# Small constants on another queue at the start, and the last tokens ahead of the feed-forward weights

## The chip, the cores and the metric

The kernel runs on one core of one Trainium2 chip. The metric is the device time of one launch in microseconds (us); lower is better. All tensors are float32. The core has five engines that each work through their own list of instructions in order: TensorE (PE in profiles), VectorE (DVE), ScalarE (ACT), GpSimd (POOL) and SyncE (SP), which here only issues transfers (DMAs). DMAs issued by SP and by ScalarE and by GpSimd stand in three queues; in the profile these are q1 (SP), q10 (ScalarE) and q0 (GpSimd).

## The reference

The input x has 4 sequences of 1024 tokens with 512 channels. Four blocks follow one another, each added to its input:

```python
x = x + mixer_a(layernorm(x))     # 16 heads of 64, state 64
x = x + ffn(layernorm(x))
x = x + mixer_b(layernorm(x))     # 64 heads of 16, state 128
x = x + ffn(layernorm(x))         # the same weights again
```

A mixer is a state-space layer: a projection (`in_proj_w`) gives a gate z, the channels that go through a causal convolution of four taps (weights `conv_w`, bias `conv_b`) and one dt for each head. With `A = -exp(A_log)` and `dt = softplus(dt + dt_bias)` a decaying state is carried along the sequence; `D` times the channel is added, the result is gated, normalized with the weight `norm_w`, and projected by `out_proj_w`.

The feed-forward block, cut to its core, is

```python
x_norm  = layer_norm(x, in_gamma, in_beta)
thought = x_norm[:, -1, :] @ agg_w + agg_b              # the last token of each sequence
for _ in range(4):
    t = layer_norm(thought, pn_gamma, pn_beta)
    t = gelu(t @ d1_w + d1_b)
    thought = thought + (t @ d2_w + d2_b)
broadcast = (thought @ bc_w + bc_b)[:, None, :]
gate = sigmoid(x @ gate_w + gate_b)                      # all tokens
out = layer_norm(x + gate * broadcast, out_gamma, out_beta)
```

So a chain of small products on four rows (the thought) stands beside a large product on all 4096 tokens (the gates), and the result needs both.

## The kernel before, in words

The tokens are cut into 32 items of 128 (NT). `mixer` (L188) takes them in groups of two (256 tokens), and is called twice, for a and for b; `ffn` (called 0 and 1 below) is called after each. Between them the activations go through DRAM (`xa`, `xb`).

**The mixer's start.** At L221 to L242 the weights and constants are loaded. `load_big` (L136) issues a weight in pieces, by turns on SP and on GpSimd. For w_in these are five cuts of columns: the first, third and fifth on SP, the others on GpSimd. Then SP issues the small constants one after the other: cw (convolution weights, L225), cb (their bias, L227), nw (norm weight, L229), dtb (dt bias, L231), Ab (A_log given to all partitions, L233), and Dc (D, L236 to L239), whose rows are given to the partitions with a last dimension that is strided in DRAM: 1024 pieces of four bytes, in two DMAs for mixer a and eight for b. w_out (L242, 2 MB) and the x of later groups follow on SP. VectorE then scales cw and cb (L244, L245), limits Ab (L247), ScalarE takes its exponential (L248), VectorE multiplies it (L249), and w_out is scaled with nw in eight instructions (L252).

**The order in a mixer.** The instructions of PE, DVE, ACT and POOL are laid out by hand under `tc.manual_schedule`: the norm of the first group (L373 to L413: statistics, scaling xn on ScalarE, transposes tpx on TensorE, copies into xnT on ScalarE), then `front` of the first group (products pz for the gate z and pd for dt, pc for the channels, all L324 or L480; the convolution L451 on VectorE), then chunk by chunk with the next group's front dealt out between. The transfers on SP and everything in `ffn` are put in order by the scheduler of the language, from the program's own order and its cost estimates. DMAs issued by SP and ScalarE share eight completion semaphores in turn, so that a DMA is issued only when the one eight before it in that turn has landed.

**The feed-forward part.** The order of its text is the order of its priorities. L1012 to L1029 name the loads: gw (gate weights, on GpSimd), the rows gb, agb, d2b, gam, bet, bcb (on GpSimd, helper `row`, L1002), the columns ing, inb, png, pnb, d1b (on SP, helper `col`, L1007), agg (SP), d1 in four pieces of 512 columns by turns on SP and GpSimd, and d2 in two halves (d2a on SP, d2b_w on GpSimd). After the helpers comes the chain: xl, the last token of each of the four sequences, is loaded in four DMAs (L1080 to L1082), normalized twice, transposed (tpl), scaled with ing and inb, and multiplied by agg (`split_project`, L1053, agg_ps, then the sum over the partitions sum_agg). Four thought steps follow (L1092: tpt, d1_ps, hr, tph, Gelu, d_ps, sum_d). `gate(i)` (L1129) makes the gate of one item: xn, transposes tpg, copy xnT, product g_ps (L1141), sg. ffn 0 makes all 32 gates and stores them; its last part is done in mixer b, in `last_step`. ffn 1 makes 12 gates ahead, then bc_ps (L1162), the row hb through DRAM to hbc on all partitions, and for each item the last step (L1183 to L1196), with a further gate after each.

Of the kernel before, what the change touches and what calls it, by code (L numbers as in the profile page):

```python
# [8 lines left out]
F32 = mybir.dt.float32  # L9
# [6 lines left out]
P = 128  # L16
GC = 2
GT = GC * P
D = 512
KD = D // P  # L20
E = 1024
KE = E // P
FF = 2048
KF = FF // P
# [48 lines left out]
def hybrid_kernel(  # L73
# [37 lines left out]
    nc = tc.nc  # L111
    NB, S, _ = x.shape
    NCH = S // P
# [5 lines left out]
    wts = ctx.enter_context(tc.tile_pool(name="wts", bufs=1))  # L119
# [16 lines left out]
    def load_big(tag, shape, src, name, parts):  # L136

        t = wts.tile(shape, F32, tag=tag, name=name)
        v = src.rearrange("(k p) n -> p k n", p=P)
        for i, (k0, k1, n0, n1) in enumerate(parts):  # L140
            eng = nc.sync if i % 2 == 0 else nc.gpsimd
            eng.dma_start(t[:, k0:k1, n0:n1], v[:, k0:k1, n0:n1])
        return t
# [44 lines left out]
    def mixer(m, in_w, conv_w, conv_b, dt_bias, A_log, Dv, norm_w, out_w, src, dst, first, stats, last_step=None):  # L188
        NH, HD, N = m.heads, m.head, m.state
# [18 lines left out]
        with stack:  # L208
            wk = stack.enter_context(tc.tile_pool(name=f"wk_{m.name}", bufs=1, reuse_waits="tile"))
# [5 lines left out]
            def mm(name):  # L215
# [5 lines left out]
            w_in = load_big(  # L221
                "w1", [P, KD, m.cols], in_w, f"w_in_{m.name}", [(0, KD, n0, n1) for n0, n1 in cuts]
            )
            cw = wk.tile([P, m.tiles, TAPS], F32, tag="cw", name=f"cw_{m.name}")
            nc.sync.dma_start(cw, conv_w)  # L225
            cb = wk.tile([P, m.tiles], F32, tag="cb", name=f"cb_{m.name}")
            nc.sync.dma_start(cb, conv_b)  # L227
            nw = wk.tile([P, KE], F32, tag="nw", name=f"nw_{m.name}")
            nc.sync.dma_start(nw, norm_w)  # L229
            dtb = wk.tile([P, NH], F32, tag="dtb", name=f"dtb_{m.name}")  # L230
            nc.sync.dma_start(dtb, dt_bias.partition_broadcast(P))  # L231
            Ab = wk.tile([P, NH], F32, tag="Ab", name=f"Ab_{m.name}")
            nc.sync.dma_start(Ab, A_log.partition_broadcast(P))  # L233

            Dc = wk.tile([P, KE], F32, tag="Dc", name=f"Dc_{m.name}")
            d_heads = Dv.rearrange("(e h) -> h e", h=HT)  # L236
# [709 lines left out]
            with tc.manual_schedule(  # L946
# [13 lines left out]
                for n in range(len(groups)):  # L960
                    if n + 2 < len(groups):
                        fs.append(Group(*groups[n + 2]))
                    f, ahead, behind = (fs + [None, None])[n : n + 3]
# [22 lines left out]
    def ffn(r, src, dst, stats):  # L986
# [4 lines left out]
        with stack:  # L991
            wk = stack.enter_context(tc.tile_pool(name=f"wk_f{r}", bufs=1, reuse_waits="tile"))
# [9 lines left out]
            def row(src, tag, parts=P, pool=wk):  # L1002
                t = pool.tile([parts, D], F32, tag=tag, name=f"{tag}_{r}", bufs=1)
                nc.gpsimd.dma_start(t, src.partition_broadcast(parts))
                return t

            def col(src, tag, n):  # L1007
                t = wk.tile([P, n], F32, tag=tag, name=f"{tag}_{r}")
                nc.sync.dma_start(t, src)
                return t  # L1010

            d2_rows = d2_w.rearrange("(s r) n -> s r n", s=2)  # L1012
            w_d2b = wk.tile([P, KF // 2, D], F32, tag="d2b_w", name=f"d2b_w_{r}")
            w_agg = wk.tile([P, KD, D], F32, tag="aggbc", name=f"agg_{r}")
            gw = wk.tile([P, KD, D], F32, tag="gw", name=f"gw_{r}")
            nc.gpsimd.dma_start(gw, gate_w.rearrange("(k p) n -> p k n", p=P))
            gb = row(gate_b, "gb")
            ing, inb = col(in_gamma, "ing", KD), col(in_beta, "inb", KD)
            agb, d2b = row(agg_b, "agb", NB), row(d2_b, "d2b", NB)
            png, pnb = col(pn_gamma, "png", KD), col(pn_beta, "pnb", KD)  # L1020
            d1b = col(d1_b, "d1b", KF)
            nc.sync.dma_start(w_agg, agg_w.rearrange("(k p) n -> p k n", p=P))
            w_d1 = load_big("w1", [P, KD, FF], d1_w, f"d1_{r}", [(0, KD, q * D, (q + 1) * D) for q in range(FF // D)])
            w_d2 = [load_big("w2", [P, KF // 2, D], d2_rows[0], f"d2a_{r}", [(0, KE, 0, D)])]
            nc.gpsimd.dma_start(w_d2b, d2_rows[1].rearrange("(k p) n -> p k n", p=P))
            w_d2.append(w_d2b)
# [50 lines left out]
                nc.tensor.matmul(ps[:NB], sums, rows, start=True, stop=True)  # L1077
                return ps[:NB]

            xl = wk.tile([NB, D], F32, tag="row", name=f"xl_{r}")  # L1080
            for b in range(NB):
                nc.sync.dma_start(xl[b : b + 1, :], src[b * NCH + NCH - 1][P - 1 : P, :])  # L1082
            for n, eps in enumerate((1e-5, 1e-6)):
                normalize(xl, xl, layer_stats(sm, xl, eps, "l", f"l{n}_{r}"))
            tx = tnT[:, :, :NB]
# [7 lines left out]
            for s in range(4):  # L1093
                tag = f"{r}_{s}"
# [117 lines left out]

    stats = [pp.tile([P, NT, 3], F32, tag="stats", name=f"stats_{r}") for r in range(2)]
    mixer(MIX_A, a_in_w, a_conv_w, a_conv_b, a_dt_bias, a_A_log, a_D, a_norm_w, a_out_w, streams[0], streams[1], first_x, stats[0])
    step = ffn(0, streams[1], None, stats[0])
    mixer(MIX_B, b_in_w, b_conv_w, b_conv_b, b_dt_bias, b_A_log, b_D, b_norm_w, b_out_w, streams[1], streams[2], [], stats[1], step)
    ffn(1, streams[2], streams[3], stats[1])


# [65 lines left out]
```

## Time and profile before

| What | Before |
|---|---|
| Time, median of 3 runs | 3233.39 us (3232.75 to 3239.16) |
| The profiled execution's own time | 3234.7 us |
| Its span in the profile | 3233.0 us |
| Mean granted TensorE clock | 0.965 of full speed |
| TensorE busy | 2890.7 us, 89% |
| VectorE busy | 2035.7 us, 63% |
| ScalarE busy | 1246.2 us, 39% |
| GpSimd busy | 782.5 us, 24% |
| Bytes moved by DMA | 135.97 MB, mean 42 GB/s |

In the profile the stages lie as follows: mixer a to about 1228 us, ffn 0 to about 1420, mixer b to about 2962, ffn 1 to the end. Each line of the timeline gives the start, the duration, the engine, the source line, the instruction with what it writes and reads, how many of them stand in a row, and in brackets how long the engine was idle before and what released it. A line of transfers ("SPq") times only the issue on the engine's queue, not the transfer. The table of stretches gives the busy time of each engine in each stretch, so that one sees in each stage which engine is full. TensorE's records overlap a little[...].

### The profile page before, as it was taken

The numbers are of one execution on the slowest core, as the hardware profiler recorded it, in microseconds if no ns is written. First come the engines' busy times: TensorE is split into PE (matmuls) and PEld (weight loads), VectorE is DVE, ScalarE is ACT, GpSimd is POOL, SyncE is SP. The second block draws the span as 40 slices with busy tenths as digits, with TensorE's granted clock in tenths as the row PEclk, the third lists the DMA queues.
The fourth block names the chain that finished last, engine by engine and source line by source line (L and its number), as shares of the span: only waits on it lengthen the run. The fifth ranks groups of instructions, "written<-read, shape, count | busy, mean of one in ns | idle before, by whom it ended". The sixth has DMA issues, their size and how long they took to land. (4 is left out here: it accounts for less than half of the span.)

```text
span 3233.0 us, 48622 instructions
## 1 busy us (share of the span) xinstructions
PE 2890.7 (89%) x18372; PEld 1916.6 (59%) x18372; DVE 2035.7 (63%) x4326; ACT 1246.2 (39%) x2848; POOL 782.5 (24%) x842
## 2 busy tenths in 40 slices
PE   6999999999999988988999888989888989997973
PEld 5666666666666653356666666666666666664331
DVE  4666566655556642267766687776687676674288
ACT  2333333333333323334443444344444444343242
POOL 1122121122211221022222223221222222221068
PEclk9999999999999998999999999999999999998987
DMA  3000000000000025420000000000000000023143
GB/s 110 15 16 15 16 16 16 22 16 16 15 16 22 16 67 176 168 86 12 29 19 25 19 26 24 19 22 22 19 25 22 17 25 19 22 68 125 33 147 117
DMA packets 100521, 135.97 MB, mean 42 GB/s; under 512 B 40792, under 2 KB 44376, under 8 KB 100288
## 3 DMA queue, kind: packets, MB, share of 16 engines
q1 hardware_dynamic: 86944, 100.92, 10.1%
q10 hardware_dynamic: 9216, 16.78, 1.4%
q0 software_dynamic: 4128, 15.16, 1.3%
q8 instruction: 146, 2.39, 0.3%
q14 instruction: 87, 0.71, 0.1%
HBM read 96.09 MB, written 36.72 MB: 41 GB/s over the span
## 5 line engine op out<-in xcount | busy, mean ns | idle before, releaser
L324 PE MATMUL pc_b<-xnT_b,w_in_b 128*128 128x259 f32 x1280 | 360.3, 408 | 22.2 <-DVE u_b L451 22.2
L786 DVE TENSOR_TENSOR L_b<-L_b,Gm_b 128x1024 f32<-128x1024 f32 x256 | 317.4, 1282 | 2.9 <-ACT L_b L779 2.9
L646 PE MATMUL pout_a<-w_out_a,h_a 128*128 128x512 f32 x512 | 285.6, 650 | 27.3 <-DVE u_a L451 27.3
L324 PE MATMUL pc_a<-xnT_a,w_in_a 128*128 128x259 f32 x1152 | 309.2, 393 | 0.0
L324 PE MATMUL pz_a<-xnT_a,w_in_a 128*128 128x256 f32 x1024 | 300.2, 407 | 8.9 <-ACT xnT_a L413 8.9
L324 PE MATMUL pz_b<-xnT_b,w_in_b 128*128 128x256 f32 x1024 | 292.4, 394 | 0.7 <-ACT xnT_b L413 0.7
L324 PEld LDWEIGHTS pc_b<-xnT_b,w_in_b 128*128 128x128 f32 x1280 | 230.7, 201 | 101.6 <-issue 37.3
L1141 PE MATMUL g_ps<-gw,xnT_f 128*128 128x512 f32 x512 | 253.2, 639 | 39.4 <-ACT xnT_f L1138 25.5
L779 ACT ACTIVATE L_b<-seg_b 128x512 f32<-128x512 f32 x512 | 262.7, 598 | 65.9 <-PE seg_b L772 65.1
L646 PE MATMUL pout_b<-w_out_b,h_b 128*128 128x512 f32 x512 | 278.5, 635 | 0.0
L451 DVE SCALAR_TENSOR_TENSOR u_b<-pc_b,cw_b,u_b 128x256 f32<-128x256 f32 x480 | 231.7, 483 | 70.7 <-ACT u_b L447 59.3
L802 PE MATMUL py_b<-L_b,hdt_b 128*32 128x128 f32 x4096 | 162.7, 294 | 118.0 <-DVE L_b L786 116.7
L451 DVE SCALAR_TENSOR_TENSOR u_a<-pc_a,cw_a,u_a 128x256 f32<-128x256 f32 x432 | 208.3, 482 | 53.0 <-ACT u_a L447 41.6
L324 PEld LDWEIGHTS pc_a<-xnT_a,w_in_a 128*128 128x128 f32 x1152 | 193.3, 190 | 68.5 <-issue 22.9
L802 PEld LDWEIGHTS py_b<-L_b,hdt_b 128*32 128x32 f32 x4096 | 109.5, 115 | 161.7 <-issue 81.7
L1141 PEld LDWEIGHTS g_ps<-gw,xnT_f 128*128 128x128 f32 x512 | 97.4, 201 | 169.2 <-issue 116.4
L324 PEld LDWEIGHTS pz_a<-xnT_a,w_in_a 128*128 128x128 f32 x1024 | 168.6, 193 | 47.1 <-ACT xnT_a L413 9.3
L447 ACT ACTIVATE u_a<-pc_a,cb_a,cw_a 128x256 f32<-128x256 f32 x144 | 81.3, 564 | 283.9 <-PE pc_a L324 220.3
L324 PEld LDWEIGHTS pz_b<-xnT_b,w_in_b 128*128 128x128 f32 x1024 | 166.3, 190 | 37.1 <-issue 18.2
L854 POOL TENSOR_TENSOR h_b<-h_b,z_b 128x256 f32<-128x256 f32 x128 | 90.6, 729 | 386.4 <-ACT sq_b L853 386.4
L824 DVE TENSOR_TENSOR yo_a<-po_a,ea_a 128x512 f32<-128x512 f32 x56 | 36.1, 686 | 220.4 <-PE po_a L820 220.4
L647 PEld LDWEIGHTS ssq_a<-ones,sq_a 128*128 128x128 f32 x512 | 98.4, 194 | 127.8 <-issue 115.9
(310 smaller groups left out, 5275.3 us busy)
## 6 DMA issues: line engine op xcount, KB each, us to landing
x_f<-xa SPq DMA_DIRECT2D x32, 256.0 KB
sgd<-sg SPq DMA_DIRECT2D x32, 256.0 KB
sgl<-sgd SPq DMA_DIRECT2D x32, 256.0 KB
x_b<-xa SPq DMA_DIRECT2D x32, 256.0 KB
xb<-x_b ACTq DMA_DIRECT2D x32, 256.0 KB
x_f<-xb SPq DMA_DIRECT2D x32, 256.0 KB
x_g<-xb SPq DMA_DIRECT2D x32, 256.0 KB
out<-x_g SPq DMA_DIRECT2D x32, 256.0 KB
```

The lines of the kernel that those rows point to most:

```text
L324: nc.tensor.matmul(*args, **kw)
L447: nc.scalar.activation(u, ps[:, 0:GT], AF.Identity, bias=cb[:, j : j + 1], scale=cw[:, j, 0:1])
L451: nc.vector.scalar_tensor_tensor(u, ps[:, k : k + GT], cw[:, j, k : k + 1], u, ALU.mult, ALU.add)
L646: nc.tensor.matmul(pout, f.hs[e // 2][:, e % 2, cols], w_out[:, e, :], **on)
L647: nc.tensor.matmul(ssq[:, 0:1], sqs[e // 4][:, e % 4, :], ones[:, 0:1], **on)
L779: nc.scalar.activation(L[:, r], sg[r0 + r], AF.Exp)
L786: nc.vector.tensor_mul(Lr, Lr, Gm.unsqueeze(1).to_broadcast([P, 2 * HB, P]))
L802: nc.tensor.matmul(py[cg * CT : (cg + 1) * CT, e % 4, :], hdt[:, h // HC, u : u + HC, :], Ls[half][:, r, hq, :], start=not started[cg], st ...
L824: nc.vector.tensor_mul(heads_of(tmp), heads_of(po), over_head(el[:, half * HALF : (half + 1) * HALF], P, HALF))
L854: nc.gpsimd.tensor_mul(yh, yh, zs[half * 2 + r][:, :, cols])
L1141: nc.tensor.matmul(ps, xnT[:, k, :], gw[:, k, :], start=(k == 0), stop=(k == KD - 1))
```

## The change

In the mixer, Ab, cw, cb and dtb are issued first of the constants and in this order; for mixer a (`first`) they are issued by ScalarE, for mixer b by SP. nw, Dc and w_out stay where they were on SP. In `ffn`, d1 is loaded in two halves, both on SP, and named first; then gw, then the four xl loads (before, at the head of the chain), agg, and the rows and columns; d2 and the rest follow as before.

```diff
+            q = nc.scalar if first else nc.sync
+            Ab = wk.tile([P, NH], F32, tag="Ab", name=f"Ab_{m.name}")
+            q.dma_start(Ab, A_log.partition_broadcast(P))
             cw = wk.tile([P, m.tiles, TAPS], F32, tag="cw", name=f"cw_{m.name}")
-            nc.sync.dma_start(cw, conv_w)
+            q.dma_start(cw, conv_w)
             cb = wk.tile([P, m.tiles], F32, tag="cb", name=f"cb_{m.name}")
-            nc.sync.dma_start(cb, conv_b)
+            q.dma_start(cb, conv_b)
+            dtb = wk.tile([P, NH], F32, tag="dtb", name=f"dtb_{m.name}")
+            q.dma_start(dtb, dt_bias.partition_broadcast(P))
             nw = wk.tile([P, KE], F32, tag="nw", name=f"nw_{m.name}")
             nc.sync.dma_start(nw, norm_w)
-            dtb = wk.tile([P, NH], F32, tag="dtb", name=f"dtb_{m.name}")
-            nc.sync.dma_start(dtb, dt_bias.partition_broadcast(P))
-            Ab = wk.tile([P, NH], F32, tag="Ab", name=f"Ab_{m.name}")
-            nc.sync.dma_start(Ab, A_log.partition_broadcast(P))
...
+            v_d1 = d1_w.rearrange("(k p) n -> p k n", p=P)
+            w_d1 = wts.tile([P, KD, FF], F32, tag="w1", name=f"d1_{r}")
+            for n0 in range(0, FF, FF // 2):
+                nc.sync.dma_start(w_d1[:, :, n0 : n0 + FF // 2], v_d1[:, :, n0 : n0 + FF // 2])
+            gw = wk.tile([P, KD, D], F32, tag="gw", name=f"gw_{r}")
+            nc.gpsimd.dma_start(gw, gate_w.rearrange("(k p) n -> p k n", p=P))
+            xl = wk.tile([NB, D], F32, tag="row", name=f"xl_{r}")
+            for b in range(NB):
+                nc.sync.dma_start(xl[b : b + 1, :], src[b * NCH + NCH - 1][P - 1 : P, :])
+            w_agg = wk.tile([P, KD, D], F32, tag="aggbc", name=f"agg_{r}")
+            nc.sync.dma_start(w_agg, agg_w.rearrange("(k p) n -> p k n", p=P))
+            gb = row(gate_b, "gb")
+            agb, d2b = row(agg_b, "agb", NB), row(d2_b, "d2b", NB)
+            ing, inb = col(in_gamma, "ing", KD), col(in_beta, "inb", KD)
+            png, pnb = col(pn_gamma, "png", KD), col(pn_beta, "pnb", KD)
+            d1b = col(d1_b, "d1b", KF)
             d2_rows = d2_w.rearrange("(s r) n -> s r n", s=2)
             w_d2b = wk.tile([P, KF // 2, D], F32, tag="d2b_w", name=f"d2b_w_{r}")
-            w_agg = wk.tile([P, KD, D], F32, tag="aggbc", name=f"agg_{r}")
-            gw = wk.tile([P, KD, D], F32, tag="gw", name=f"gw_{r}")
-            nc.gpsimd.dma_start(gw, gate_w.rearrange("(k p) n -> p k n", p=P))
-            gb = row(gate_b, "gb")
-            ing, inb = col(in_gamma, "ing", KD), col(in_beta, "inb", KD)
-            agb, d2b = row(agg_b, "agb", NB), row(d2_b, "d2b", NB)
-            png, pnb = col(pn_gamma, "png", KD), col(pn_beta, "pnb", KD)
-            d1b = col(d1_b, "d1b", KF)
-            nc.sync.dma_start(w_agg, agg_w.rearrange("(k p) n -> p k n", p=P))
-            w_d1 = load_big("w1", [P, KD, FF], d1_w, f"d1_{r}", [(0, KD, q * D, (q + 1) * D) for q in range(FF // D)])
...
-            xl = wk.tile([NB, D], F32, tag="row", name=f"xl_{r}")
-            for b in range(NB):
-                nc.sync.dma_start(xl[b : b + 1, :], src[b * NCH + NCH - 1][P - 1 : P, :])
```

In the order that the scheduler lays out, SP issues at the start of mixer a x, the three w_in cuts, nw, Dc twice, w_out and then the next x; ScalarE issues Ab, cw, cb and dtb before its table load and takes the exponential of Ab before xn. In mixer b, ScalarE's exponential of Ab comes between the two copies into xnT, where it came after both. In both feed-forward parts SP still issues d1 at the end of the mixer, and then d2a, the four xl, agg, ing, inb, png, pnb, d1b, where it was d2a, the five columns, agg, xl. gw keeps its place on GpSimd.

## The prediction

> **What bounds the kernel now.** I read the table of stretches first, because the change touches only the start of the kernel and the ends of its mixers. Its columns are the stretch, then busy microseconds (count) of TensorE, its weight loads, VectorE, ScalarE and GpSimd, the granted clock, the DMA share and GB/s.
>
> ```profile
> 0.00:20.00 20.00, 1.97 (x8) 1.57 (x8) 5.97 (x38) 3.39 (x4) 5.25 (x15) 1.00 0.82 279
> 20.00:40.00 20.00, 19.17 (x73) 16.57 (x74) 5.93 (x17) 2.43 (x6) 0.00 (x0) 1.00 0.43 159
> 40.00:60.00 20.00, 12.38 (x60) 9.86 (x58) 17.76 (x54) 9.29 (x20) 1.40 (x4) 0.96 0.00 0
> 60.00:80.00 20.00, 20.00 (x103) 15.19 (x102) 7.10 (x17) 7.91 (x21) 1.90 (x1) 0.87 0.04 8
> 1340.00:1360.00 20.00, 20.00 (x59) 8.99 (x58) 3.46 (x5) 7.37 (x13) 0.00 (x0) 1.00 0.77 281
> 1420.00:1440.00 20.00, 18.53 (x95) 16.07 (x96) 18.41 (x58) 9.89 (x17) 2.76 (x2) 1.00 0.09 19
> 3020.00:3040.00 20.00, 19.66 (x121) 6.77 (x124) 5.64 (x15) 4.53 (x8) 0.54 (x1) 1.00 0.05 14
> 3200.00:3220.00 20.00, 0.00 (x0) 0.00 (x0) 17.95 (x30) 3.88 (x5) 17.10 (x15) 0.50 0.40 132
> ```
>
> TensorE sets the pace of both mixers and of the first feed-forward part. Exceptions: before 20 us nearly nothing runs; from 38 to 60 us VectorE does; at 1420 to 1480 VectorE does; and after 3080, when the thought chain is done, VectorE and GpSimd do. Next, the timeline of the start (start, duration, engine, line, work, idle before and what released it):
>
> ```profile
> 8.89 0.22 DVE L394 SCALAR_TENSOR_TENSOR mv_a<-mv_a 128x1 f32<-128x1 f32 x2
> 19.18 0.18 DVE L244 TENSOR_SCALAR cw_a<-cw_a 128x36 f32<-128x36 f32 x1 [10.07 <-DMA cw_a<-in_L_attn_a_conv_w]
> ...
> 35.26 3.26 DVE L252 TENSOR_SCALAR w_out_a<-w_out_a,nw_a 128x512 f32<-128x512 f32 x8 [2.89 <-DMA w_out_a<-in_L_attn_a_out_proj_w]
> 38.44 2.94 DVE L451 SCALAR_TENSOR_TENSOR u_a<-pc_a,cw_a,u_a 128x256 f32<-128x256 f32 x6
> ```
> ```profile
> 11.10 0.59 ACT L413 COPY xnT_a<-tpx_a 128x512 f32<-128x512 f32 x1 [0.50 <-PE tpx_a L411]
> 20.09 0.21 ACT L248 ACTIVATE Ab_a<-Ab_a 128x16 f32<-128x16 f32 x1 [8.40 <-DVE Ab_a L247]
> ```
> ```profile
> 7.90 4.05 SPq L233 DMA_DIRECT2D Ab_a<-in_L_attn_a_A_log x1
> 11.99 3.66 SPq L238 DMA_DIRECT2D Dc_a<-in_L_attn_a_D x2
> 19.00 0.39 SPq L142 DMA_DIRECT2D w_out_a<-in_L_attn_a_out_proj_w x1
> ```
>
> Two waits stand in a row. The small constants land only at 19 us, behind w_in; ScalarE's exponential of Ab stands between its two copies into xnT, so TensorE's first pz starts at 20.83. Then w_out lands at 35.26, and its eight scalings stand before the first convolution on VectorE, which therefore starts at 38.44 and is what the stretch to 60 us runs on.
>
> **Startup.** Ab, cw, cb and dtb move to ScalarE's queue ahead of its table load; nothing is added or removed. VectorE's order becomes Ab, statistics of x, cw, aggregate, cb, ..., so its set-up stands behind cb. SP issued three such loads in 0.45 to 1.10 us each and x_first took 2.9 us from issue (0.81) to use (3.72), so with w_in running beside it I put cb at 5 to 7 us. From 4.66 to 9.11 VectorE has 4.45 us of set-up plus 0.2 for Ab: L394 ends at 9.7 to 11.7. From there to both copies done takes 3.6 us (9.1 to about 12.5 without the exponential): TensorE starts at 13.3 to 15.3, 5.5 to 7.5 earlier.
>
> Here the Trainium skill is weighed ("DMA: Bandwidth & Descriptors"). "Rules for kernel authors" speaks against the change: loads spread over SP, ACT and GpSimd gain no bandwidth, only issue time. Then the constants would land as w_in drains, at 17.5, TensorE would start no earlier than before (17.5 + 4.65 + 3.6 = 25.7), and z would be ready at 37.2, hardly ahead of 38.44: gain about 1 us at most. "Queues, rings and completion order" says that each engine takes its rings in turn. The row decides for the latter, since GpSimd's and SP's queues did share from 8 to 12 us:
>
> ```profile
> q0 software_dynamic: 261, 1.02, 66.2%
> q1 hardware_dynamic: 266, 0.54, 36.7%
> ```
>
> But the first convolution still needs w_out, which stays on SP behind w_in and Dc. SP's issues freeze when all the loads in flight have not landed (a load waits for the eighth before it, and Ab's took 4.05 us to get in); w_out was issued only at 19.00, because the load eight before it was w_in's last. Now that place is cb's, so w_out goes out at about 7 us, and Dc at 6 to 7 instead of 12. Dc is 1024 pieces of four bytes. The same page's rule that a strided last dimension becomes one descriptor per element agrees, and would only name a cost; its size is in the trace, as packets in 19 to 22 us (first) and in 1428 to 1430 us, where Dc of mixer b has the queue to itself:
>
> ```profile
> DMA packets 283, 0.00 MB, mean 0 GB/s; under 512 B 283, under 2 KB 283, under 8 KB 283
> ...
> DMA packets 238, 0.00 MB, mean 0 GB/s; under 512 B 238, under 2 KB 238, under 8 KB 238
> ```
>
> That is 94 to 119 per us, 8.6 to 10.9 us for 1024. Yet in 17 to 18 us 946 small packets passed in one us, when w_in had just drained. So the slow part is making the pieces, not moving them, and it ran on behind w_in from 12 us. Started at 6.5 it ends at 15 to 17.5, about when w_in drains; w_out's 2 MB follow in 5.3 us (at the 390 GB/s of 8 to 12 us), plus some 2 us to land: 24 to 27, I take 26. If instead the pieces are only worked off once w_in is gone, w_out lands at about 34. I take 26 for the burst at 17 us; both ends stay in the range. First convolution: the later of w_out + 3.2 (35.26 to 38.44) = 29.2 and z done (TensorE's start + 10.85 + 0.7 = 24.9 to 26.9). So 29.2 against 38.44: **-9** (ends -11 and -1). It is kept to the end: VectorE is busy 17.8 of 20 us after its first convolution and in the same order, and TensorE saturates after that. The next x loads land behind w_out at about 28 and are first used 6 us after the first convolution (44.38 before), so they hide; third w_in waits for Ab's landing, hidden too since its columns are needed 15 us after TensorE's start.
>
> **First feed-forward part.** Both halves of d1 now go on SP (before, half on GpSimd at 0.8 us of issue each, with nothing behind them that waited). The sums' round trips through DRAM are all issued before d1, so nothing urgent is behind it. xl goes straight after d2a, then agg, then the five small constants; the last xl waits for the last store of the mixer (issued 1229.79), so agg is issued near 1232 as before. inb now waits for d2a's landing (about 1241) and is used at about 1256. The thought chain starts some 4 us earlier, but TensorE is busy 20 of 20 us up to 1380 with the same products: **0** (-1 to +1.5).
>
> **Start of mixer b.** Ab first on SP; ScalarE now does copy, table load (1.28), exponential, copy, so pz starts near 1424.3 instead of 1422.8. VectorE, with 18.4 of 20 busy, hides 1.5 us and saves waits of 0.91 and 0.33: **-0.3** (-0.9 to +1.5 if that cover is gone).
>
> **Second feed-forward part.** TensorE, one bc product, and the tail:
>
> ```profile
> 2975.42 16.27 PE L1141 MATMUL g_ps<-gw,xnT_f 128*128 128x512 f32 x32 [5.50 <-DMA gw<-in_L_ffn_gate_w]
> 2992.80 0.41 PE L1051 MATMUL tpl<-ident,xl 4*128 4x4 f32 x4 [1.12 <-DVE xl L184]
> ...
> 3071.13 3.60 PE L1162 MATMUL bc_ps<-bc,thT 128*4 128x512 f32 x8
> ```
>
> gw's load stays where it was. xl was issued at 2976.46, after d2a had landed; now at about 2964, so its norm runs before the gates' products finish and tpl comes near 2989. The same products then stand between the steps as before. Waits of TensorE for the chain go: 1.12 (tpl), 1.70, 0.28 and 0.34 (at later steps), 0.68 (3070.07), and one gate product of 0.95 moves behind bc: 5.1 at most, of which I count those that my step by step sum kept: bc ends at 3070.8 instead of 3074.7, **-3.9** (-1 to -4; the tail's different interleaving of gates and items adds -2 to +6 at its ends). The tail is bound by VectorE and GpSimd and starts when hbc lands, so it moves along.
>
> **Sum.** -9 + 0 - 0.3 - 3.9 = -13.2 from the profiled execution's 3234.7 us gives 3221.5. The median of the runs, 3233.39, is 1.3 lower: **3220.2**. The measurement can tell 0.2%, 6.5 us.
>
> **Rivals.** (1) w_out takes the place of the constants: it lands at 34, the startup gives 1 and the sum is -5.2: 3228. For it: Dc and w_out keep their places on one ring, and w_out's packets came staggered from 23 to 28 us. Against it: the burst at 17 us. (2) The thought chain was hidden: gates on TensorE fill what it leaves, ffn 1 gives 0, total -9.3: 3224. For it: 19.7 of 20 busy at 3020. Against: the waits named end on the chain. (3) Slower: VectorE's new order in the tail. Gates and items are interleaved otherwise over 32 items in 157 us, 4.9 us each, of which VectorE's own work is about 4. A wait on GpSimd's add of 0.4 us for each item costs 13 and cancels everything; from 0.6 each (+19) it is 3240. For it: GpSimd is as busy as VectorE there. Against: the counts are the same, and only some neighbours swap.
>
> **How the numbers follow.** As forecast 0.58, rival 1 0.20, rival 2 0.12, rival 3 0.10. Range: the startup's -11 with -6 in ffn 1 is 3215, rounded down to 3213; the startup's -1 with ffn 1 at 0 and the two positive bounds (+3) is 3235. Faster by over 0.2% needs under 3227: most of the first and third cases, 0.68. Rival 1 and part of rival 3 lie within 0.2%: 0.21. Slower 0.11.
>
> **What would show it.** Right: cw used before 7 us, pz from 13 to 15, L252 at 24 to 27, first convolution near 29, the full TensorE stretch beginning near 51; agg before 2991 and hbc's first use near 3076 less the earlier gains. Wrong: L252 still after 32 (rival 1), bc not moving against the end of mixer b (rival 2), or more than 157 us between hbc and the end (rival 3).

## The result, and the profile after

| | Before | After |
|---|---|---|
| Median of 14 runs each, on one chip | 3236.72 us (3232.28 to 3242.47) | 3237.01 us (3231.5 to 3243.62) |
| The profiled execution's own time | 3234.7 us | 3234.81 us |
| Its span | 3233.0 us | 3233.1 us |
| Mean granted TensorE clock | 0.965 | 0.963 |

The ratio after to before is 1.0002, with a 95% interval of 0.9994 to 1.0009: no difference. The forecast of 3220.2 us is missed by 17 us, and the range, which ended at 3235, by two.

The forecast's first term was 9 us at the start. These are lines of VectorE's timeline of the kernel after, in the columns explained above:

```profile
7.95 0.17 DVE L247 TENSOR_SCALAR cb_a<-cb_a 128x9 f32<-128x9 f32 x1 [1.82 <-DMA cb_a<-in_L_attn_a_conv_b]
...
12.25 0.22 DVE L396 SCALAR_TENSOR_TENSOR mv_a<-mv_a 128x1 f32<-128x1 f32 x2
...
26.80 0.69 DVE L520 SCALAR_TENSOR_TENSOR z_a<-tz_a,pz_a 128x512 f32<-128x512 f32 x1 [0.21 <-ACT tz_a L515]
35.66 3.26 DVE L254 TENSOR_SCALAR w_out_a<-w_out_a,nw_a 128x512 f32<-128x512 f32 x8 [8.17 <-DMA w_out_a<-in_L_attn_a_out_proj_w]
38.83 2.95 DVE L453 SCALAR_TENSOR_TENSOR u_a<-pc_a,cw_a,u_a 128x256 f32<-128x256 f32 x6
```

In the kernel before, z's line was this:

```profile
31.68 0.69 DVE L518 SCALAR_TENSOR_TENSOR z_a<-tz_a,pz_a 128x512 f32<-128x512 f32 x1 [0.32 <-ACT tz_a L513]
```

The constants do arrive early: cb is used at 7.95 (before at 19.36), and z starts at 26.80 (before at 31.68). But the scaling of w_out starts at 35.66 where it started at 35.26, and the first convolution at 38.83 where it was 38.44. The bracket at L254 tells why: the 2.89 us for which VectorE waited for w_out before have become 8.17 us. What TensorE won at the front, VectorE lost in front of w_out. ScalarE's and SP's queues in the same stretch:

```profile
1.74 0.45 ACTq L231 DMA_DIRECT2D cb_a<-in_L_attn_a_conv_b  x1
...
5.18 0.21 ACT L250 ACTIVATE Ab_a<-Ab_a 128x16 f32<-128x16 f32 x1 [1.14 <-DVE Ab_a L249]
```
```profile
5.93 5.02 SPq L240 DMA_DIRECT2D Dc_a<-in_L_attn_a_D  x2
10.99 0.76 SPq L142 DMA_DIRECT2D w_out_a<-in_L_attn_a_out_proj_w  x1
11.80 16.93 SPq L133 DMA_DIRECT2D x_a<-in_L_attn_a_x  x4
```

ScalarE's exponential of Ab is done at 5.4 instead of 20.3. SP begins to issue the two Dc loads at 5.93 instead of 11.99, as forecast, and issues w_out at 10.99 instead of 19.00 (forecast about 7). w_out lands as late as before all the same. The table of stretches shows the same in sums (busy us of TensorE, its weight loads, VectorE, ScalarE and GpSimd with their counts, clock, DMA share, GB/s):

```profile
0.00:20.00 20.00, 6.02 (x21) 5.08 (x22) 5.77 (x39) 4.19 (x6) 5.24 (x15) 1.00 0.80 279
20.00:40.00 20.00, 20.00 (x78) 17.12 (x79) 5.31 (x14) 1.72 (x3) 0.00 (x0) 1.00 0.44 159
40.00:60.00 20.00, 10.55 (x42) 7.87 (x41) 17.80 (x55) 9.29 (x20) 1.40 (x4) 0.81 0.00 0
1420.00:1440.00 20.00, 16.94 (x71) 14.32 (x72) 16.30 (x50) 7.68 (x14) 3.32 (x4) 0.74 0.09 19
```

TensorE now works 6.02 us in the first 20 (before 1.97) and 20.00 in the next, but from 40 to 60, where VectorE sets the pace with 17.80 us as before, it only has less left to do. The last row is the start of mixer b: a clock of 0.74 where it was 1.00, and 16.94 us of TensorE where there were 18.53. The clock is taken up below, under "Mixer b's constants in their old order". The first convolution slipped from 1432.69 to 1436.00 (the kernel before first, then after):

```profile
1432.69 1.52 DVE L451 SCALAR_TENSOR_TENSOR u_b<-pc_b,cw_b,u_b 128x256 f32<-128x256 f32 x3
```
```profile
1436.00 1.52 DVE L453 SCALAR_TENSOR_TENSOR u_b<-pc_b,cw_b,u_b 128x256 f32<-128x256 f32 x3 [1.30 <-ACT u_b L449]
```

TensorE's lines, before and after, and then ScalarE's after show where the slip begins:

```profile
1422.78 0.70 PE L324 MATMUL pz_b<-xnT_b,w_in_b 128*128 128x256 f32 x2 [0.68 <-ACT xnT_b L413]
```
```profile
1424.89 1.22 PE L326 MATMUL pz_b<-xnT_b,w_in_b 128*128 128x256 f32 x2 [2.35 <-ACT xnT_b L415]
```
```profile
1421.54 0.59 ACT L415 COPY xnT_b<-tpx_b 128x512 f32<-128x512 f32 x1 [0.17 <-PE tpx_b L413]
1422.14 1.28 ACT L250 ACT_TABLE_LOAD   x1
1424.10 0.26 ACT L250 ACTIVATE Ab_b<-Ab_b 128x64 f32<-128x64 f32 x1 [0.68 <-DVE Ab_b L249]
1424.27 0.57 ACT L415 COPY xnT_b<-tpx_b 128x512 f32<-128x512 f32 x1
```

pz starts 2.35 us after TensorE's last work (before: 0.68), because the table load and the exponential of Ab stand between the two copies into xnT, and the exponential waits for Ab's landing besides.

In the second feed-forward part the chain did come earlier, on TensorE's timeline:

```profile
2976.63 13.61 PE L1148 MATMUL g_ps<-gw,xnT_f 128*128 128x512 f32 x26 [5.23 <-DMA gw<-in_L_ffn_gate_w]
2990.17 0.41 PE L1061 MATMUL tpl<-ident,xl 4*128 4x4 f32 x4
...
3069.57 3.60 PE L1169 MATMUL bc_ps<-bc,thT 128*4 128x512 f32 x8
```

tpl no longer waits for xl (before 1.12 us) and starts at 2990.17 instead of 2992.80, bc at 3069.57 instead of 3071.13. From the result row hb on, though, the end comes later: from hb to the end of the span it took 158.2 us before and takes 159.9 now. The last items show new waits of GpSimd (POOL) and VectorE, here the kernel before and then after:

```profile
3217.63 1.71 POOL L1190 TENSOR_TENSOR sg<-o,sg 128x512 f32<-128x512 f32 x1
3224.04 1.71 POOL L1190 TENSOR_TENSOR sg<-o,sg 128x512 f32<-128x512 f32 x1 [0.34 <-DVE sg L1183]
```
```profile
3220.25 1.76 POOL L1197 TENSOR_TENSOR sg<-o,sg 128x512 f32<-128x512 f32 x1 [1.29 <-DVE mv_o L179]
...
3222.05 0.69 DVE L176 BATCH_NORM_STATS2 st_o<-sg 128x6 f32<-128x512 f32 x1 [1.15 <-POOL sg L1197]
...
3224.14 1.76 POOL L1197 TENSOR_TENSOR sg<-o,sg 128x512 f32<-128x512 f32 x1 [1.62 <-DVE mv_o L179]
...
3225.93 0.69 DVE L176 BATCH_NORM_STATS2 st_o<-sg 128x6 f32<-128x512 f32 x1 [1.15 <-POOL sg L1197]
```

The adds of GpSimd wait 1.29 and 1.62 us for VectorE, and VectorE's statistics then 1.15 us twice for the add. In the kernel before, the same two adds had waited not at all and 0.34 us, and VectorE's statistics behind them not at all: the gate of the first was scaled one item earlier (L1183 at 3214.22; now L1190 at 3219.52), and between the scaling of the second and its statistics VectorE had two large instructions to do where it now has one.

So each part moved something, and the sum is nothing. On the profiled executions, the chain from the end of mixer b to hb takes 109.6 us instead of 112.6. hb comes only 1.6 us earlier (3073.20 for 3074.76), so mixer b ended 1.4 us later than before. With the 1.7 us that the tail loses, the sum is +1.4 - 3.0 + 1.7 = +0.1, the difference of the spans. The +1.4 is that of one pair of executions and proves little: e4 below, whose mixers are those of the kernel before, ended mixer b 4.5 us earlier than it (2957.66 for 2962.19).

### The profile page after: what moved, and what is told of

Read it like the earlier page. It is cut to its first block, busy times and chain, and to the rows that moved or that the text cites. A ratio compares the mean times of both kernels' runs of the same rounds, so it can differ in the third digit from the quotient of the medians.

```text
span 3233.1 us, 48646 instructions
## 1 busy us (share of the span) xinstructions
PE 2895.3 (90%) x18372; PEld 1921.3 (59%) x18372; DVE 2033.6 (63%) x4326; ACT 1245.9 (39%) x2848; POOL 778.0 (24%) x838
```

## The experiments

Each kernel was timed beside the kernel before on the same chip; the chips of e1 to e4, e5 to e8 and e9 and e10 differ, so ratios compare and medians do not. "Store" is the issue of the first store of xa, at 121.36 in the trace of before and at 122.40 after: a mark just behind the start of mixer a. How good the two marks are is seen in kernels with the same start: before and e4 differ by 1.25 us in the first convolution and 1.5 in the store, e1, e6 and e7 by up to 1.4 and 2.9. So the convolution is good to about 1.5 us and the store to about 3. In the expectations A stands for the theory that I held when they were written, B for its rival.

| Kernel | Median, us (runs) | Ratio to before, 95% | First convolution | Store |
|---|---|---|---|---|
| after | 3237.01 (14) | 1.0002 [0.9994, 1.0009] | 38.83 | 122.40 |
| e1_wout_first | 3224.70 (5) | 0.9965 [0.9952, 0.9979] | 29.86 | 112.77 |
| e2_dc_act | 3230.63 (21) | 0.9988 [0.9980, 0.9995] | 33.88 | 117.20 |
| e3_b_as_before | 3237.24 (13) | 1.0003 [0.9994, 1.0011] | 38.83 | 121.89 |
| e4_ffn_alone | 3236.28 (13) | 1.0000 [0.9990, 1.0009] | 37.19 | 119.83 |
| e5_wout_alone | 3234.88 (22) | 0.9992 [0.9985, 0.9999] | 37.52 | 120.73 |
| e6_combined | 3228.07 (5) | 0.9965 [0.9951, 0.9978] | 30.29 | 114.04 |
| e7_tail | 3227.13 (5) | 0.9956 [0.9941, 0.9971] | 28.93 | 111.18 |
| e8_dc_rows | 3231.64 (10) | 0.9971 [0.9960, 0.9981] | 30.78 | 112.86 |
| e9_sp_first | 3229.31 (8) | 0.9969 [0.9956, 0.9981] | 29.44 | 112.92 |
| e10_scale_pool | 3228.53 (6) | 0.9965 [0.9952, 0.9978] | 28.10 | 113.98 |

### w_out ahead of Dc

```diff
             nc.sync.dma_start(nw, norm_w)
+            w_out = load_big("w2", [P, KE, D], out_w, f"w_out_{m.name}", [(0, KE, 0, D)])
             Dc = wk.tile([P, KE], F32, tag="Dc", name=f"Dc_{m.name}")
...
-            w_out = load_big("w2", [P, KE, D], out_w, f"w_out_{m.name}", [(0, KE, 0, D)])
```

> The changed kernel with w_out issued on SP ahead of Dc instead of behind it. Theory A (Dc's 1024 four-byte pieces stand ahead of w_out on SP's ring and hold it): w_out follows w_in directly, so VectorE's scaling of w_out starts at 24 to 27 us instead of 35.66 and the first convolution at 28 to 30 instead of 38.83. The next x loads now stand behind Dc and may cost 1 to 3 us of that again at about 35. Total 5 to 9 us below the changed kernel. Theory B (w_out is late for its own sake: its rows, or bandwidth): scaling still starts after 31 us, total unchanged.

VectorE's timeline of this kernel:

```profile
26.01 0.17 DVE L490 TENSOR_TENSOR v_a<-pd_a,dtb_a 128x16 f32<-128x16 f32 x1 [4.21 <-PE pd_a L482]
26.10 3.25 DVE L254 TENSOR_SCALAR w_out_a<-w_out_a,nw_a 128x512 f32<-128x512 f32 x8
29.26 0.68 DVE L520 SCALAR_TENSOR_TENSOR z_a<-tz_a,pz_a 128x512 f32<-128x512 f32 x1
29.86 2.95 DVE L453 SCALAR_TENSOR_TENSOR u_a<-pc_a,cw_a,u_a 128x256 f32<-128x256 f32 x6
```

w_out is there when VectorE comes to it. The convolution starts 8.6 us earlier than before, the store comes 8.6 us earlier, and the median is lower by 0.35%, that is 11 us with an interval of 7 to 16: more than the 5 to 9 expected, but not told apart from 8.6. The next x is used at 35.81 without a wait, so its place behind Dc cost nothing there. The transfers of single microseconds show the mechanism. First the kernel after from 18 to 19 and from 20 to 21 us:

```profile
DMA packets 553, 0.08 MB, mean 82 GB/s; under 512 B 528, under 2 KB 528, under 8 KB 553
```
```profile
DMA packets 101, 0.00 MB, mean 0 GB/s; under 512 B 101, under 2 KB 101, under 8 KB 101
```

And the kernel with w_out first from 20 to 21 and from 25 to 26 us:

```profile
DMA packets 190, 0.39 MB, mean 389 GB/s; under 512 B 0, under 2 KB 0, under 8 KB 190
```
```profile
DMA packets 107, 0.01 MB, mean 9 GB/s; under 512 B 103, under 2 KB 103, under 8 KB 107
```

In the kernel after, w_in has drained at 18, then there is one burst of 528 small packets (128 of them rows of nw, the rest of four bytes), and then about 100 per us, which move next to nothing: spread evenly over 16 engines that would be one piece per 150 ns for each. w_out's packets only begin to come at 22 us and reach 400 GB/s at 30. With w_out first, its rows go at 385 to 389 GB/s directly behind w_in, and the slow pieces come after it, when nobody needs them yet.

### Dc on ScalarE's queue

```diff
-                nc.sync.dma_start(
+                q.dma_start(
                     Dc[h * HD : (h + 1) * HD, :], d_heads[h : h + 1, :].to_broadcast([HD, KE])
```

> The changed kernel with mixer a's Dc issued by ScalarE behind the four constants, so that SP carries only x, w_in, nw and w_out. Theory A (what counts is the ring on which the pieces stand): scaling of w_out starts at 24 to 27 us, first convolution 28 to 30, next x loads not held, total 8 to 10 us below the changed kernel. Theory B (small pieces slow the engines whatever the ring): w_out lands after 31 us, total unchanged within 3 us.

VectorE's timeline:

```profile
30.11 3.26 DVE L254 TENSOR_SCALAR w_out_a<-w_out_a,nw_a 128x512 f32<-128x512 f32 x8 [3.15 <-DMA w_out_a<-in_L_attn_a_out_proj_w]
```

The result lies in the middle: scaling at 30.11 with 3.15 us of waiting, the store 4.2 us earlier, the time 0.12% lower. On another queue the pieces no longer stand in front of w_out, but they still run beside w_in and w_out and take their turns on the same engines: from 16 to 22 us the trace has 35 to 120 small packets in each microsecond, and 215 to 338 GB/s instead of the 370 to 396 of the kernel with w_out first.

### w_out ahead of Dc, without the change

The same edit as in the first experiment, made to the kernel before.

> The kernel before with one change: w_out issued on SP ahead of Dc. The constants still go on SP behind w_in. Theory A (two waits in a row, and each one alone hides the other): w_out lands near 24 to 26 us, TensorE still starts near 21, z is done near 32.4, the eight scalings follow it, and the first convolution starts at 35 to 36 us: a gain of 2.5 to 3.5 us, a third of what both together give (8.6). Theory B (only w_out matters, the constants' move is worth nothing): first convolution near 30 as with both.

VectorE's timeline:

```profile
20.00 0.18 DVE L244 TENSOR_SCALAR cw_a<-cw_a 128x36 f32<-128x36 f32 x1 [11.12 <-DMA cw_a<-in_L_attn_a_conv_w]
...
21.95 0.17 DVE L247 TENSOR_SCALAR Ab_a<-Ab_a 128x16 f32<-128x16 f32 x1 [1.60 <-DMA Ab_a<-in_L_attn_a_A_log]
...
33.75 0.69 DVE L518 SCALAR_TENSOR_TENSOR z_a<-tz_a,pz_a 128x512 f32<-128x512 f32 x1 [0.21 <-ACT tz_a L513]
34.35 3.25 DVE L252 TENSOR_SCALAR w_out_a<-w_out_a,nw_a 128x512 f32<-128x512 f32 x8
37.52 1.52 DVE L451 SCALAR_TENSOR_TENSOR u_a<-pc_a,cw_a,u_a 128x256 f32<-128x256 f32 x3
```

The wait for w_out is gone (no bracket at L252), but the constants still arrive only from 20.00 on, z can start only at 33.75, and the scaling stands behind z. The convolution gains 0.9 us, less than expected (2.5 to 3.5), and the time is lower by 0.08% [0.01%, 0.15%]. The rest of the 2.89 us went into z itself, which came 2.07 us later than before: Ab was usable only at 21.95 instead of 19.88. In the packets, w_out's rows run beside the last rows of dtb and Ab from 17 to 21 us; that they held them up is likely, but no run isolates it.

With e1 this completes a square: the constants' move alone changes the convolution by +0.4, w_out's move alone by -0.9, both within what kernels with the same start differ by, and both together by -8.6. The two waits stood one behind the other in front of the same instruction. Moving the one that ended first (the constants) could give nothing, and moving the one that ended last (w_out) at most the 2.89 us between their ends.

### Dc without pieces

```diff
+            if first:
+                Dall = wk.tile([P, NH], F32, tag="Dall", name=f"Dall_{m.name}")
+                q.dma_start(Dall, Dv.partition_broadcast(P))
+                for h in range(HT):
+                    part = slice(h * HD, (h + 1) * HD)
+                    nc.gpsimd.tensor_copy(Dc[part, :], Dall[part].rearrange("p (e h) -> p h e", h=HT)[:, h, :])
+            else:
...
```

w_out keeps its place behind Dc's in SP's list; for mixer a Dc now comes as whole rows of 64 bytes on ScalarE's queue.

> The changed kernel, w_out in its place, but mixer a's Dc made from whole rows: D is loaded to all partitions in rows of 64 bytes on ScalarE's queue and two GpSimd copies pick the heads, so that the 1024 four-byte pieces are gone. Theory A (it is the pieces that hold w_out back): scaling of w_out starts by 26 us, first convolution near 29.9, total as with w_out ahead of Dc (3222 to 3228). Theory B (w_out is held by its own place behind w_in): scaling after 31 us.

```profile
27.02 3.25 DVE L261 TENSOR_SCALAR w_out_a<-w_out_a,nw_a 128x512 f32<-128x512 f32 x8
30.78 2.95 DVE L460 SCALAR_TENSOR_TENSOR u_a<-pc_a,cw_a,u_a 128x256 f32<-128x256 f32 x6
```

w_out is in time here too, at 27.02 where 26 was expected, and the store comes 8.5 us earlier. The median lies above the expected 3222 to 3228, but so does this chip's kernel before (3238.17), and the ratio, 0.9971, is not told apart from e1's. In e2 the same load stood on the same queue as pieces, and gave 4.2. So the trouble is neither w_out's place in the list nor the queue in itself, but the pieces of four bytes. The Trainium skill has this as a rule ("DMA: Bandwidth & Descriptors", "Rules for kernel authors"): a strided last dimension costs one descriptor for each element, so rearrange the load to be contiguous. The prediction cited it and thought that it only named a cost; here it was worth 8 us at the first convolution (30.78 for 38.83).

### The constants on SP, ahead of w_in

```diff
+            if first:
+                q = nc.sync
+                Ab = wk.tile([P, NH], F32, tag="Ab", name=f"Ab_{m.name}")
+                q.dma_start(Ab, A_log.partition_broadcast(P))
...
             w_in = load_big(
```

With w_out ahead of Dc as in e1; cw, cb and dtb follow Ab in the same way.

> The changed kernel with w_out ahead of Dc, and mixer a's four constants on SP again, but issued ahead of w_in instead of on ScalarE's queue. Theory A (what helps is standing ahead of w_in, not the queue): constants land by 5 us, set-up ends before 11, w_in comes some 2 us later; TensorE starts at 13.5 to 16, first convolution 28 to 31, total as with w_out ahead of Dc on ScalarE's queue (ratio 0.995 to 0.998 to the kernel before). Theory B (the other queue is needed, since anything ahead of w_in on SP holds up the weights that bound the start): first convolution after 32.5.

```profile
7.11 0.17 DVE L258 TENSOR_SCALAR cb_a<-cb_a 128x9 f32<-128x9 f32 x1
...
26.27 3.26 DVE L265 TENSOR_SCALAR w_out_a<-w_out_a,nw_a 128x512 f32<-128x512 f32 x8 [0.62 <-DMA w_out_a<-in_L_attn_a_out_proj_w]
29.44 2.96 DVE L464 SCALAR_TENSOR_TENSOR u_a<-pc_a,cw_a,u_a 128x256 f32<-128x256 f32 x6
```

cb is used at 7.11 and the convolution starts at 29.44, no later than with ScalarE's queue (8.28 and 29.86 in e1), and the ratios 0.9969 and 0.9965 are not told apart. It is the place ahead of the big weight that counts, and not the other queue.

### The scalings of w_out on GpSimd

```diff
-                nc.vector.tensor_scalar_mul(w_out[:, e, :], w_out[:, e, :], nw[:, e : e + 1])
+                (nc.gpsimd if first else nc.vector).tensor_scalar_mul(w_out[:, e, :], w_out[:, e, :], nw[:, e : e + 1])
```

> The changed kernel with w_out ahead of Dc, and mixer a's eight scalings of w_out on GpSimd instead of VectorE. Theory A (of the first convolution's 29.9 us, 3.3 are the scalings that stand before it on VectorE): first convolution at 26.5 to 27.5 us, total 1 to 3 us lower than with the scalings on VectorE. Theory B (GpSimd, slower, delays the power for the next group's statistics that is queued behind the scalings, or slows VectorE beside it): first store of mixer a not earlier than 112.8 us, total the same or worse.

GpSimd's timeline of this kernel:

```profile
24.89 12.79 POOL L254 TENSOR_SCALAR w_out_a<-w_out_a,nw_a 128x512 f32<-128x512 f32 x8 [13.23 <-DMA w_out_a<-in_L_attn_a_out_proj_w]
37.65 1.09 POOL L170 TENSOR_TENSOR mv_a<-mv_a,neg_half 128x1 f32<-128x1 f32 x2
```

Here w_out's landing is seen directly: at 24.89, inside the 24 to 27 that the prediction had hoped for. The convolution comes at 28.10, 1.8 us earlier than in e1 but later than the 26.5 to 27.5 expected, since VectorE now waits 1.26 us for ScalarE's u. The eight scalings take 12.79 us on GpSimd instead of 3.25 on VectorE, and the small power for the next group's statistics stands behind them, until 37.65; VectorE waits 1.45 us for it. The store comes 1.2 us later than in e1, within the spread of that mark, and the time is the same.

### Mixer b's constants in their old order

The kernel after, with the new order of the constants only for mixer a (`if first:`), the old one for b.

> The changed kernel with mixer b's constants in the old order, so that ScalarE's exponential of Ab comes after both copies into xnT. Theory A (the exponential between the copies keeps TensorE idle long enough that its clock is halved, which makes the first products slow): the first gate products of mixer b take 0.65 to 0.70 us a pair again instead of 1.2, the first convolution of mixer b follows the first pz by 10 us instead of 11.1 and comes 3.3 us earlier (near 1433), total 1.5 to 3.5 us below the changed kernel. Theory B (the loss there comes from the feed-forward part's new order before it): first convolution of mixer b stays near 1436, total unchanged.

TensorE's and VectorE's timelines:

```profile
1422.08 1.22 PE L339 MATMUL pz_b<-xnT_b,w_in_b 128*128 128x256 f32 x2 [0.68 <-ACT xnT_b L428]
1423.41 1.17 PE L339 MATMUL pz_b<-xnT_b,w_in_b 128*128 128x256 f32 x2
```
```profile
1432.39 1.52 DVE L466 SCALAR_TENSOR_TENSOR u_b<-pc_b,cw_b,u_b 128x256 f32<-128x256 f32 x3 [0.50 <-ACT u_b L462]
```

The gap in front of pz is 0.68 us again, and the convolution comes at 1432.39 instead of 1436.00. But the pairs of pz still take 1.22 and 1.17 us, as after, and not 0.65 as before: the clock is halved here as well, without the stall. My explanation, that the stall had brought the clock down, is wrong; in the kernel after the clock falls at 1421.17, before the stall begins at 1422.5.

The clock records of the traces show what goes with it. In all twelve traces the clock changes only on a grid of 3.41 us. At full clock, it fell to half after 363 stretches of this grid and stayed after 9739 (up to 3080 us of each trace). TensorE was busy for less than 51% of the stretch in 360 of the 363, and for 51% or more in 9699 of the 9739. TensorE's idle time ahead of the group's first transposes is 2.21 us before as after. After, all of it lies in one stretch (1417.76 to 1421.17, busy for 1.20 of 3.41 us, 35%); before, the edge at 1420.12 cuts it in two, and TensorE is busy for 54% and 61% of the stretches on either side. In e5, with mixer b's old order and the old `ffn`, the clock fell as well, for 3.4 us. So the lower clock in the row of 1420 to 1440 comes from where the grid happened to lie, as far as these traces show, and not from the new order; the stall then kept it low longer, 10.2 us in five of the six kernels with the new order where it was 6.8 in e3, e6 and e7.

From the first transposes of the group to the first convolution there are 12.0 us in the kernel before and in e5, and 12.2 in the kernel with the feed-forward edit alone; 12.65 to 12.8 in three kernels with the old order at half clock (e3, e6, e7); and 15.0 to 15.5 in six with the new order, also at half clock (after, e1, e2, e8, e9, e10). So the order costs about 2.6 us at this place, and the clock somewhat under 1. The median did not move (1.0003 against 1.0002): 2.6 us is less than 0.1%, and the intervals are twice as wide.

### The feed-forward edit alone

The kernel before, with only the new order of loads in `ffn`.

> The kernel before with only the feed-forward parts changed. Theory A (their chain gains and is spent again in the tail): tpl and the result row hb come 2 to 4 us earlier in ffn 1 counted from the end of mixer b, the end within 1.5 us of the kernel before's: total 0 to -2 us. Theory B (the chain's gain reaches the end): -3 to -5 us.

From the end of mixer b to hb it takes 109.4 us (before 112.6), from hb to the end 160.1 (before 158.2). Both parts of the effect belong to this edit; 3.2 us are won in the chain, 1.9 are given back in the tail, and the time is the same. The kernel e5, with the old `ffn`, has 158.3 in the tail; all kernels with the new one have 159.9 to 160.3.

### Both good orders together, and the tail

e6 is e1 with mixer b's old order. For e7 the scaling of the gate with hbc starts one item earlier for each of the last three items:

```diff
+                    if NT - 4 <= i < NT - 1:
+                        begin(i + 1)
+                    for _ in items[i]:
...
```

> The changed kernel with w_out ahead of Dc and with mixer b's constants in the old order. If the two parts add: first convolution of mixer a near 29.9, of mixer b 13 us after its first transpose instead of 15.5, total 2 to 3.5 us below the kernel with w_out ahead of Dc alone (3224.7), so near 3222. If mixer b gains its late start back later, total equals that kernel's.

> The combined kernel, and in ffn 1 the scaling with hbc of each of the last three items is started ahead of the rest of the item before it. Theory A (the 1.8 us that the tail lost lie in the last three items, where GpSimd's add now waits for VectorE's late scaling): from hb to the end 158.0 to 158.6 us instead of 160, the last three items 9 us instead of 10.9, total 1.5 to 2 us lower. Theory B (the loss is spread over the tail): hb to the end stays near 160.

e6 has its first convolution at 30.29 and 12.8 us at mixer b's start; its ratio is e1's, so the 2 to 3.5 us more that were expected if the parts add are not seen, nor could five runs exclude them. In e7 the last three items take 9.3 us instead of 10.9, as hoped, but the time is lost in front of them, in two of the scalings that were started earlier:

```profile
3204.44 1.66 DVE L1203 SCALAR_TENSOR_TENSOR sg<-sg,hbc 128x512 f32<-128x512 f32 x1
...
3210.21 1.65 DVE L1203 SCALAR_TENSOR_TENSOR sg<-sg,hbc 128x512 f32<-128x512 f32 x1
```

Up to 3204.44 VectorE's lines of e6 and e7 agree to 0.02 us, counted from hb. In e6 the same scalings take 0.65 to 0.66 us each; here these two fall beside adds of GpSimd and take 1.0 us longer each. From hb to the x_g instruction (L1216) at which the last three items are counted, e7 needs 146.62 us where e6 needs 144.64, and the whole tail 160.3: nothing is won. Which order would give the 1.7 us back stays open. The fastest kernels are e1, e6, e7, e8, e9 and e10, 0.29 to 0.44% below before and not told apart.

## Why the prediction was wrong

**Startup, -9: failed.** The step was "Started at 6.5 it ends at 15 to 17.5, about when w_in drains", from the 946 small packets in 17 to 18 us. That was misread. The trace has the size of each packet: 566 of the 946 were rows of 32 to 144 bytes, those of cw, cb, nw, dtb and Ab, five loads of 128 rows that stood on SP ahead of Dc; 380 had four bytes. In two microseconds, 17 to 19, it is 517 of four bytes in the kernel before; after, from 18 to 20, it is 507. Each load leaves 16 packets of four bytes when it lands (on SP's queue 48 by 11 us, for three loads, before Dc was issued), so about 420 of the first and 475 of the second were Dc's. With w_out first it is about 417, from 23 to 25 us behind w_out. So when the load ahead has drained, about as many of Dc's 1024 pieces are ready whether its two halves were issued at 11.99 and 15.04 us (before) or at 5.93 and 6.78 (after): the making of the pieces did not run on behind w_in for as long as the prediction let it. What stops it is not seen in the trace. The rest comes at some 100 per us, and w_out behind it. The prediction had "only worked off once w_in is gone, w_out lands at about 34" as its other end (35.66), which is rival 1, at a chance of 0.20; its total, 3228, was missed as well, by the terms that follow. One count would have decided it: 946 packets against the 640 rows that stood ahead of Dc.

**What was right in it.** The constants behind w_in were one wait, w_out the other; z done 11.55 us after TensorE's start (11.54); the convolution at w_out plus 3.2 (3.17); w_out at 24 to 27 if nothing stood ahead of it (24.89 in e10), and the gain kept to the store (e1). cb at 7.95 missed its 5 to 7, pz at 15.95 its 13.3 to 15.3, and z, done at 27.49, its 24.9 to 26.9, because VectorE waits 1.82 us for cb with all its set-up behind. Of the two rules weighed, the turn-taking of rings held for the constants (they landed beside w_in), and e9 shows that another queue was not needed for it.

**First feed-forward part, 0: right.** tpl came 2.9 us earlier (1255.81 for 1258.67), and the last gate at 1418.5 as before.

**Start of mixer b, -0.3 (at most +1.5): wrong.** The stall was seen, its cover was not there: "VectorE, with 18.4 of 20 busy, hides 1.5 us". VectorE was busy, but with work that the first convolution stands behind anyway; it then waited 0.81 us for pd and 1.30 for ScalarE's u. About 2.6 us were lost, outside the bound, which left out that the exponential also waits for Ab's landing (1.14 us at L249). That the clock fell there was chance, as far as the traces show; it adds somewhat under 1.

**Second feed-forward part, -3.9: half right.** The chain's gain measured 3.0. The tail's bound of -2 to +6 was set, but it was counted at nothing in the sum; it measured +1.7. Net -1.3. It is rival 3's mechanism, but not at 0.6 us for every item: it strikes the last three items alone.

**Sum.** Expected were -9, 0, -0.3 and -3.9. Measured were +0.4 at the first convolution, 0, about +2.6 at mixer b's start and -1.3 in the second feed-forward part. Of the two losses the one pair of profiles keeps +1.4 at the end of mixer b, and the forecast's 13 us are gone. The range's upper end, 3235, took the second feed-forward part at 0 and left out the +6 that the text itself gave the tail; with it the range would have reached to about 3240.

## What to carry to other kernels

When two waits end one after the other in front of the same instruction, moving the first alone gives nothing, and moving the second alone at most the time between their ends; count more only for moving both, and look for what else stands ahead on the ring of the second. Loads of single elements belong behind every load that is needed soon, or should be turned into rows; a burst of small packets is only evidence for one load when the rows of the others are subtracted. A change of order in a stage that two engines share (here the tail) is not to be counted at nothing before its new neighbours have been followed.

## What the runs showed of the hardware

- Four-byte pieces on one queue passed at about 100 to 120 per us at first (after from 19 us, e1 from 24), and held up the rows behind them; on another queue (e2, 16 to 22 us) they ran beside the rows, which moved at 215 to 338 GB/s instead of 370 to 396.
- The granted clock of TensorE changed only on a grid of 3.41 us, and fell to half after stretches of it in which TensorE was busy for less than about 51% (360 of 363 falls; 9699 of the 9739 stretches without a fall were at 51% or more). At the start of mixer b it was half for 3.4 to 10 us in ten of the twelve profiles.
- At the start of the kernel a pair of pz also takes 1.20 us, as at half clock in mixer b, although the table's clock column says 1.00: the traces have no clock record there, their first is at 30.9 us before, 28.5 after and 36.6 in e5. At full clock the pair takes 0.65.
- In the tail, VectorE's instructions on 128x512 take 0.65 to 0.75 us alone and 1.6 to 1.75 us when they start beside an add of GpSimd (after: L1203 took 1.75 at 3212.68, where an add ran from 3212.47, and 0.73 at 3226.54, where none ran). The Trainium skill has a reason for this ("SBUF — State Buffer", "Who interferes with whom": a VectorE instruction with two inputs from SBUF and a GpSimd instruction that reads SBUF exclude one another). The times agree, and in e7 two scalings that came to lie beside such adds took 1.65 instead of 0.66; that this is the cause no run here isolates.
